# A transformer decoder on one core: rotary products read from PSUM, layernorm's step on ScalarE, a re-priced plan, and the token shift by SBUF-to-SBUF transfers

## The chip, the cores and the metric

The kernel runs on one core of one Trainium2 chip. The metric is the device time of one execution in microseconds. Before the change the median of three runs is 1289.61 us (1286.52 to 1293.66). The profile is one further execution, which took 1292.12 us, with a span of 1290.3 us from its first to its last instruction.

## The reference

`x` and a context have 32 batches of 128 tokens by 128 channels, all fp32. Four stages follow one another, with a layernorm after the first, the second and the last two together:

```
x = layernorm(x + self_attention(x))              # 16 heads, keys = queries = x
x = layernorm(x + cross_attention(x, ctx))        # 16 heads of 8, band mask of width 64
x = layernorm(x + layer_1(layer_0(x)))            # two local-attention layers

def shift_token(t):                               # half of the channels one token later
    t1, t2 = split(t, 2, axis=-1)
    t2 = pad(t2, one row of zeros ahead)[:, :-1]
    return concatenate([t1, t2])

def layer(x):
    h = shift_token(x)
    q, k, v = split(h @ wqkv, 3)                  # 8 heads of 64
    q, k = l2norm(q) * qs, l2norm(k) * ks
    q, k = rotary(q, k)                           # q * cos * scale + rotate_half(q) * sin * scale
    x = x + local_attention(q, k, v) @ wo
    h = layernorm(shift_token(x)) * lg + lb
    a, g = split(h @ w1 + b1, 2)
    return x + (a * gelu(g)) @ w2 + b2
```

What the change touches is `shift_token`, used twice in each layer, the rotary step with the norms of q and k, and every layernorm.

## The kernel before

**Tiling.** The 32 batches are cut into ten groups of 2, 3, 3, 4, 4, 4, 4, 4, 3 and 1 (`SIZES`); n is the number of batches in a group. Tokens lie on the 128 partitions, so a group's tile is 128 x (n x 128) elements. Each group goes through four stages: self attention (`self_attention`), cross attention (`cross_attention`), layer 0 and layer 1 (`layer`). Each stage works batch by batch, and the stages of different groups are mixed with each other, each stage a set lag behind the one before (`LAGS`, `CLOSE`, `SPREAD`, `EARLY`).

**What sets the order.** Nothing is issued while it is described. `op` (L84) notes down an engine, a price in ns, what is read and written, and the function that emits it. At the end `Plan.issue` (L132) makes a list schedule: it keeps a clock for each engine, reckons when each ready operation could start from the prices of what it needs, and takes the operation of least number among those that can start within `NEAR` ns of the earliest. The result is one fixed order for each of the engines PE, DVE, ACT, POOL and SP. Every engine then runs its own order, waiting at each instruction for what it needs. The prices exist only in this plan; they decide the order, and nothing on the chip. Buffers come from rings (`Ring`): `m` is the eight PSUM banks, `big` and `mid` are SBUF tiles, `sm` small ones. Transfers all go through SP's queue; a transfer is priced at 1800 ns before it moves, its bytes over a rate, and 400 ns after it.

**The token shift.** `shifted` (L759), used ahead of each layer's feed-forward part, makes a shifted tile in SBUF: POOL copies the first 64 channels (L763), TensorE multiplies the other 64 by a shifted identity matrix (L767), which moves rows one partition on and puts a zero in the first, and ScalarE copies the result out of PSUM (L771). `turned_shifted` (L774), at the start of each layer, needs the shifted tile transposed. It transposes the plain tile (L373), and ScalarE copies the second half one column on (L782, L783), where a column of zeros has been set by POOL (L779).

**A local batch.** `local_batch` (L790) takes one batch through a layer's attention. TensorE makes q, k and v (L796). ScalarE copies each out of PSUM (L801) and squares q and k (L807); VectorE sums the squares (L810); POOL takes the power -1/2 (L813, L814). POOL multiplies the swapped halves by the sine table (L824), VectorE the plain ones by the cosine table (L833), adds the two (L837), and scales by the norms (L840). Transposes (L851), scores (L865, L871), maxima (L421), exponentials (L466), the division (L885, L886), transposes of the weights (L481, copied at L488), the outputs (L900) and the projection (L912) follow; L919 adds the result to x.

**Layernorm** (L377): VectorE's statistics (L382, L389), POOL's power (L397 to L400), and one scaling per batch on VectorE (L407).

**Copies of transposed weights.** `turned_half` (L475) transposes four heads and copies them out of PSUM (L488): on VectorE in cross attention, on ScalarE in the layers.

**DMAs.** Besides weights and inputs, the scores of the first two stages pass through a DRAM scratch: `in_slots` writes each batch's three bf16 parts in pieces of 256 B from 128 partitions (L518), and `stacked` reads them back as 72 rows of 4096 B (L529).

Of the kernel before, what the change touches and what calls it, by code (L numbers as in the profile page):

```python
# [28 lines left out]
AHEAD = 430  # L29
LAGS = (0, 1.35, 2.75, 4.1)  # L30
RINGS = (23, 16, 6, 4)
KEEP = (2, 3, 5)
NEAR = 0
EARLY = (0, 0.2)
CLOSE = (0.9, 0.85, 0.9, 1, 1, 1, 1.2, 1.05, 0.85, 0.95)
SPREAD = (1.4, 1.0, 0.7, 1.5)
# [40 lines left out]
class Plan:  # L77

# [51 lines left out]
    def issue(self, ahead, near=80.0, hop=60.0, table_ns=1300.0, tiling_ns=160.0, dma_ns=1800.0):  # L132
# [13 lines left out]
        def time_of(k):  # L146
            e = ops[k][0]
            return max([0.0] + [end[d] + (hop if ops[d][0] != e else 0.0) for d in ops[k][3]])
# [5 lines left out]
        shared = 0.0  # L154
# [5 lines left out]
        while len(order) < n:  # L160
            best = None
            for e in engines:
                choice, least = [], None
                for k, t in ready[e]:
                    if k > first + ahead:
                        continue
                    start = max(clock[e], t, shared if ops[k][7] else 0.0)
# [5 lines left out]
                    for vs in need.values():  # L173
                        q = vs[0].ring
                        if len(q.free) < len(vs) + (0 if q.queue[q.head] in vs else q.keep):
                            ok = False
                            break
                        start = max(start, sorted(q.free)[len(vs) - 1][0] + hop)
# [4 lines left out]
                    if e == "PE" and ops[k][8][0] != state:  # L183
                        start += tiling_ns
# [19 lines left out]
            if e == "SP":  # L204
                line = max(line, s + dma_ns) + ns
                end[k], clock[e] = line + 400.0, s + 450.0
            else:
                end[k] = clock[e] = s + ns
            if tab:
                table[e] = tab  # L210
            if port:
                shared = end[k]
# [19 lines left out]
def decoder_kernel(ctx: ExitStack, tc: tile.TileContext, a: dict, out: bass.AP):  # L232
# [35 lines left out]

    ident1 = const.tile([P, P + 1], F32, name="ident")
    ident, shift = ident1[:, 1 : P + 1], ident1[:, 0:P]  # L270
    nc.vector.memset(ident1[:, 0:1], 0.0)
# [90 lines left out]
    def turned(src, n):  # L362

        tp, t = Val(mring), Val(mid)
        op("PE", 113 * n, turn(src, tp, n), [src], [tp], hold=[t])
        op("ACT", 140 + 113 * n,
           lambda: nc.scalar.copy(t.t[:, 0 : 128 * n], tp.t[:, 0 : 128 * n]), [tp], [t])
        return t
# [8 lines left out]
    def layernorm(src, dst, n):  # L377
# [6 lines left out]
        op("DVE", n * 290, stats, [src], [st])  # L384
# [6 lines left out]
        op("DVE", n * 175, aggr, [st], [mv])  # L391
# [10 lines left out]
        op("POOL", 1100 + 260 * n, rest, [], [mv])  # L402

        def apply():
            x, y = group(src.t), group(dst.t)
            for j in range(n):
                nc.vector.tensor_scalar(  # L407
                    y[:, j, :], x[:, j, :], mv.t[:, 8 + j : 9 + j], mv.t[:, 12 + j : 13 + j],
                    ALU.mult, ALU.add,
                )  # L410

        op("DVE", 200 * n, apply, [mv] + ([src] if src is not dst else []), [dst])
# [4 lines left out]
    def maxima(s, nm):  # L417
        for b in range(2):
            op(
                "DVE", 690,  # L420
# [5 lines left out]
    def minus_max(s):  # L426
# [6 lines left out]
        def parts():  # L433
# [4 lines left out]
        op("POOL", 440, parts, [nm], [hl])  # L438
        mp = Val(mring, lambda t: t[:, 0:64].bitcast(BF16))
        op(  # L440
            "PE", 110,
# [4 lines left out]
        op("ACT", 260, lambda: nc.scalar.copy(mT.t, mp.t), [mp], [mT])  # L446
# [10 lines left out]
    def exps_of(s, sums=None):  # L457
# [4 lines left out]
        for b in range(2):  # L462
# [8 lines left out]
            op("ACT", 4 * (345 if sums else 255) + 60, exps, [s[b], (nm, b)],  # L471
# [3 lines left out]
    def turned_half(e, et, b, eng, src):  # L475
# [9 lines left out]
        op("PE", 4 * 113, pe, [src], [tp], hold=[et])  # L485
        copy = nc.vector.tensor_copy if eng == "DVE" else nc.scalar.copy
        op(eng, 690 if eng == "DVE" else 590,
# [6 lines left out]
    def in_slots(src, n, keep_src, moving):  # L494
# [4 lines left out]
        op("ACT", 140 + 113 * n,  # L499
           lambda: nc.scalar.copy(pv.t[:, 0, every], src.t[:, every]), [src], [(pv, 0)])  # L500
        op("POOL", 316 * n,
# [3 lines left out]
        op("ACT", 140 + 113 * n,  # L505
           lambda: nc.scalar.copy(pv.t[:, 1, every], rest.t[:, every]), [rest], [(pv, 1)])
        op("POOL", 316 * n,
# [26 lines left out]
    def scores_of(s, stationary, moving, hh, window=False):  # L534
# [12 lines left out]
        op("PE", 8 * 62 + 432 * window, pe,  # L547
# [22 lines left out]
    def self_half(j, hh, x0, xT, ys):  # L570
# [3 lines left out]
        for b in range(2):  # L574
# [3 lines left out]
                "PE", 875,  # L578
# [6 lines left out]
                "ACT", 590,  # L585
# [10 lines left out]
        op("PE", 8 * 60, lambda: emit_max(s, mT), [mT, (w_self, 2)], s)  # L596
        e = Val(big, heads)
        for b in range(2):
            op("ACT", 590,
# [3 lines left out]
        for k, (h0, n) in enumerate(((0, 3), (3, 3), (6, 2))):  # L603
# [9 lines left out]
            op("PE", 230 * n, pe, [e] + [(zs, i) for i in range(3)], [oz])  # L613
# [9 lines left out]
            op("DVE", 175 + 30 + 133 * n, scale, [oz], [rl, (zs, ("o", k))])  # L623

        z = lambda h0, n: zs.t[:, h0 : h0 + n, 0:D]
        for n, ns in ((4, 1270), (2, 730), (1, 450)):
# [4 lines left out]
        op("POOL", 450,  # L631
# [4 lines left out]
    def cross_attention(g):  # L636
# [9 lines left out]
        for w, src, c in ((wqT, xT, 0), (wkT, cT, 1)):  # L646
            qp, t = Val(mring), Val(mid)
            op("PE", 20 + 214 * n,
# [3 lines left out]
            op("ACT", 265 + 106 * n,  # L652
# [16 lines left out]
        op("PE", n * 228, values, [cT, w_cross], [vp], hold=[vT])  # L669
        op("ACT", 140 + 113 * n,  # L670
           lambda: nc.scalar.copy(vT.t[:, every], vp.t[:, every]), [vp], [vT])
        op("POOL", 316 * n,
# [21 lines left out]
        op("PE", n * 228, project, [onT, w_cross], [yp])  # L694
        op("DVE", 160 + 135 * n,
# [7 lines left out]
    def cross_batch(j, qs, ks, vT, on):  # L703
        vb = Val(vbring)
        op("POOL", 450,
# [5 lines left out]
        for hh in range(2):  # L711
# [4 lines left out]
            for b in range(2):  # L716
                turned_half(e, et, b, "DVE", e)
# [13 lines left out]
            op("PE", 875, pe, [et, vb], [o], hold=[oS], tiling=("columns", "columns"))  # L731
            op("ACT", 260,
# [11 lines left out]
        op("PE", 260, back, [oS], [ot])  # L744
# [11 lines left out]
        op("DVE", 560, normal, [ot], [rl, (on, j)])  # L756


    def shifted(src, n):  # L759

        h = Val(mid)
        op("POOL", 200 * n,
           lambda: nc.gpsimd.tensor_copy(group(h.t)[:, 0:n, 0:64], group(src.t)[:, 0:n, 0:64]),  # L763
           [src], [(h, 0)])
        sp = Val(mring, lambda t: t[:, 0 : 64 * n].rearrange("p (g d) -> p g d", g=n))
        op("PE", 25 + 111 * n,
           lambda: nc.tensor.matmul(  # L767
               sp.t, shift, group(src.t)[:, 0:n, 64:128], start=True, stop=True),
           [src], [sp], hold=[h])
        op("ACT", 180 + 53 * n,  # L770
           lambda: nc.scalar.copy(group(h.t)[:, 0:n, 64:128], sp.t), [sp], [(h, 1)])  # L771
        return h

    def turned_shifted(src, n):  # L774

        tp, t = Val(mring), Val(mid)
        op("PE", 113 * n, turn(src, tp, n), [src], [tp], hold=[t])
        op("POOL", 150,
           lambda: nc.gpsimd.memset(group(t.t)[64:128, 0:n, 0:1], 0.0), [], [(t, 0)])  # L779

        def act():
            nc.scalar.copy(t.t[0:64, 0 : 128 * n], tp.t[0:64, 0 : 128 * n])  # L782
            nc.scalar.copy(  # L783
                group(t.t)[64:128, 0:n, 1:P], group(tp.t)[64:128, 0:n, 0 : P - 1]
            )

        op("ACT", 280 + 225 * n, act, [tp], [(t, 1)])
        return t

    def local_batch(l, j, xin, hT, xout):  # L790
        qk = Val(big, lambda t: t[:, 0:1024].rearrange("p (a d) -> p a d", d=LD))
        vs = Val(mid, lambda t: t[:, 0:512].rearrange("p (h d) -> p h d", d=LD))
        for i in range(3):
            hp = Val(mring)
            op("PE", 875,
# [3 lines left out]
               [hT, w_layer[l]], [hp], hold=[qk if i < 2 else vs])  # L799
            op("ACT", 590,  # L800
               lambda hp=hp, i=i: nc.scalar.copy(  # L801
                   qk.t[:, LH * i : LH * (i + 1), :] if i < 2 else vs.t,
                   hp.t.rearrange("p (h d) -> p h d", d=LD)),
               [hp], [(qk, i) if i < 2 else vs])

        sq = Val(big, lambda t: t[:, 0:1024].rearrange("p (a d) -> p a d", d=LD))
        op("ACT", 1060, lambda: nc.scalar.activation(sq.t, qk.t, AF.Square), [qk], [sq])  # L807
        rn = Val(small)
        op("DVE", 1225,
           lambda: nc.vector.tensor_reduce(rn.t[:, 0:16], sq.t, AX.X, ALU.add), [sq], [rn])  # L810
# [7 lines left out]
        four = lambda t: t[:, 0:1024].rearrange("p (a h d) -> p a h d", a=2, d=LD)  # L818
        r2 = Val(big, four)

        def swap():
            q = qk.t.rearrange("p (a h) d -> p a h d", a=2)
            for d0, d1 in ((0, 32), (32, 0)):
                nc.gpsimd.tensor_tensor(  # L824
                    r2.t[:, :, :, d0 : d0 + 32], q[:, :, :, d1 : d1 + 32],
                    tabs[l][:, :, d0 : d0 + 32].unsqueeze(2).to_broadcast([P, 2, LH, 32]),
                    ALU.mult,
                )

        op("POOL", 2600, swap, [qk, w_layer[l]], [r2], port=True)  # L830
        qr = Val(big, four)
        op("DVE", 1240,
           lambda: nc.vector.tensor_tensor(  # L833
               qr.t, qk.t.rearrange("p (a h) d -> p a h d", a=2),
               tabc[l].unsqueeze(2).to_broadcast([P, 2, LH, LD]), ALU.mult),
           [qk, w_layer[l]], [qr], port=True)
        op("DVE", 1240, lambda: nc.vector.tensor_tensor(qr.t, qr.t, r2.t, ALU.add), [r2], [qr], port=True)  # L837
        op("POOL", 3200, power, [], [rn])
        op("DVE", 1240,
# [5 lines left out]
        for i in range(2):  # L845
# [9 lines left out]
            op("PE", 4 * 113, pe, [qr], [tp], hold=[qkT])  # L855
            op("ACT", 590,
# [19 lines left out]
        op("PE", 1520, scores, [qkT, (w_self, 2)], s, tiling=("whole", "rows"))  # L876
# [4 lines left out]
        for b in range(2):  # L881
# [8 lines left out]
            op("DVE", 870, divide, [], [(rl, b), (e, b)], port=True)  # L890
# [15 lines left out]
        op("PE", 875, outputs, [et, vs], [o], hold=[onT], tiling=("columns", "columns"))  # L906
        op("ACT", 590, lambda: nc.scalar.copy(onT.t[:, 0:512], o.t), [o], [onT])
# [9 lines left out]
        op("PE", 4 * 228, project, [onT, w_layer[l]], [yp], hold=[xout] if xout is not xin else [])  # L917
        op("DVE", 290,
# [4 lines left out]
    def feed_forward(l, xg, n):  # L923
        every = slice(0, 128 * n)
        h = shifted(xg, n)
        op("POOL", 316 * n,
# [6 lines left out]
        op("PE", 113 * n, turn(h, tp, n), [h], [tp], hold=[hT])  # L933
        op("DVE", 160 + 135 * n,
# [188 lines left out]
```

## Time and profile before

| | us |
|---|---|
| median of the runs | 1289.61 |
| the profiled execution | 1292.12 |
| its span | 1290.3 |

| line | engine, what | count | busy us | mean ns |
|---|---|---|---|---|
| L421 | VectorE, maxima, 512 out of PSUM | 384 | 245.6 | 681 |
| L488 | VectorE, copy of transposed weights | 128 | 82.0 | 681 |
| L488 | ScalarE, copy of transposed weights | 128 | 75.0 | 598 |
| L600 | ScalarE, exponentials, 512 out of PSUM | 128 | 70.6 | 607 |
| L466 | ScalarE, exponentials, 128 out of PSUM | 1024 | 323.0 | 399 |
| L813 | POOL, power of 16 columns | 64 | 200.8 | 3137 |
| L407 | VectorE, layernorm's step, other three row groups | 96 | 40.9 | 400 to 536 |
| L771 | ScalarE, copy of the shifted half | 20 | 7.0 | 350 |
| L782, L783 | ScalarE, the two copies of the shifted transpose | 40 | 20.0 | 504, 493 |
| L367 | ScalarE, copy of a plain transpose | 20 | 10.5 | 523 |
| L763, L779 | POOL, copy and memset of the shift | 40 | 11.4 | 478, 98 |

How to read it: a row of the profile is a group of instructions by line, engine and operation. After the operation it names the tile written and those read, the shape, and the count; then the busy time in us and the mean duration of one in ns; then the idle time of that engine just before these instructions, and what ended it. TensorE's matmul rows of fp32 stand twice for one matmul, and consecutive ones overlap, so their mean is longer than the distance from start to start. A copy's duration likewise runs a little into the next instruction. The first stretches of the span have a busy DMA (0.86 over the first 100 us); later the DMA share falls to 0.15 and under.

The DMA queue of SP carried 173792 packets and 89.67 MB, 27.5% of the time of the core's 16 DMA engines.

### The profile page before, as it was taken

Reading aid. Unit: us, or ns where it says so; the run is one execution under the profiler, and the core shown is the slowest. Engines: PE = TensorE matmul, PEld = TensorE weight load, DVE = VectorE, ACT = ScalarE, POOL = GpSimd, SP = SyncE. Lnnn points to the kernel's source line nnn. Section 1 sums busy time; section 2 is a strip of 40 time slices with the busy share of each in tenths; the row PEclk is TensorE's granted clock in tenths of the full one; section 3 lists DMA queues with packets and bytes.
Section 4 is the critical chain, followed back from the end, with each engine's and each line's share of the span. In section 5 each row is a group of like instructions: output and inputs, shape, how many; then the busy total and the mean of one; then the engine's idle time right before and its main releaser. Section 6 shows DMA issues by size and latency. Waiting matters only on the chain.

```text
span 1290.3 us, 27579 instructions
## 1 busy us (share of the span) xinstructions
PE 1213.9 (94%) x9730; PEld 888.0 (69%) x9730; DVE 1070.3 (83%) x2134; ACT 966.2 (75%) x2762; POOL 835.3 (65%) x1094
## 2 busy tenths in 40 slices
PE   7988999999979999999999999999999989999996
PEld 4766677776767865777777667778667657567664
DVE  2677889878968888887798889979899999988786
ACT  4564777777867778777778778858889968879863
POOL 2866657765857389555687468653966963786454
PEclk9999999999989999999999999999999989999999
DMA  9886414240154420732005401330300000000000
GB/s 254 209 213 193 124 39 105 56 128 9 37 136 109 99 56 1 174 89 65 20 25 138 124 1 34 94 95 18 97 2 12 18 18 2 9 1 2 2 1 25
DMA packets 173930, 91.44 MB, mean 71 GB/s; under 512 B 155872, under 2 KB 161888, under 8 KB 173536
## 3 DMA queue, kind: packets, MB, share of 16 engines
q1 hardware_dynamic: 173792, 89.67, 27.5%
q8 instruction: 77, 1.26, 0.4%
q14 instruction: 61, 0.50, 0.1%
HBM read 49.79 MB, written 39.85 MB: 69 GB/s over the span
## 4 chain that ended last, share of the span: by engine, by line
PE 45%; POOL 15%; DVE 14%; ACT 6%; issue 3%; DMA 1%; SPq 0%; POOLq 0%; DVEq 0%; ACTq 0%
PE m L796 6%; POOL sm L813 6%; PE m L481 5%; PE m L944 4%; PE m L608 4%; ACT big L466 3%; PE m L900 3%; PE m L579 3%; PE m L871 3%; PE m L912 3%; POOL big L824 3%; PE m L964 3%; PE m L724 2%; DVE sm L421 2%; PE m L542 2%
## 5 line engine op out<-in xcount | busy, mean ns | idle before, releaser
L466 ACT ACTIVATE big<-m,sm 128x128 f32<-128x128 f32 x1024 | 323.0, 399 | 54.5 <-DVE sm L421 53.9
L421 DVE TENSOR_REDUCE sm<-m 128x4 f32<-128x512 f32 x384 | 245.6, 681 | 45.4 <-PE m L871 21.5
L813 POOL TENSOR_TENSOR sm<-sm,nhalf 128x16 f32<-128x16 f32 x64 | 200.8, 3137 | 36.8 <-DVE sm L810 26.7
L628 POOL TENSOR_TENSOR big<-big 128x512 f32<-128x512 f32 (+2 forms) x192 | 163.2, 850 | 83.8 <-DVE big L618 36.8
L824 POOL TENSOR_TENSOR big<-big,layer_w 128x512 f32<-128x512 f32 x128 | 162.4, 1269 | 76.4 <-ACT big L801 71.1
L796 PE MATMUL m<-layer_w,mid 128*128 128x512 f32 x384 | 193.2, 612 | 4.2 <-DVE xb L971 2.1
L481 PE MATMUL m<-ident,big 128*128 128x128 f32 x1024 | 144.4, 276 | 15.4 <-DVE big L886 9.6
L481 PEld LDWEIGHTS m<-ident,big 128*128 128x128 f32 x1024 | 115.7, 141 | 54.9 <-issue 21.9
L579 PE MATMUL m<-self_w,mid 128*128 128x512 f32 x256 | 131.1, 626 | 7.0 <-DMA self_w<-in_self_w 5.7
L608 PEld LDWEIGHTS m<-big,big 128*128 128x128 f32 x1024 | 123.0, 191 | 13.7 <-issue 7.5
L608 PE MATMUL m<-big,big 128*128 128x129 f32 x1024 | 129.9, 276 | 0.9 <-DVE big L618 0.3
L466 ACT ACTIVATION_READ_ACCUMULATOR big<-m,sm 128x1 f32 x512 | 115.9, 226 | 0.0
L586 ACT COPY big<-m 128x512 f32<-128x512 f32 x128 | 75.1, 600 | 38.8 <-PE m L579 38.0
L618 DVE TENSOR_TENSOR big<-m,sm 128x384 f32<-128x384 f32 (+1 forms) x192 | 98.6, 514 | 6.6
L886 DVE TENSOR_TENSOR big<-big,sm 128x512 f32<-128x512 f32 x128 | 98.2, 767 | 4.6 <-DMA slots<-big 0.2
L542 PEld LDWEIGHTS <-big 72*128 72x128 bf16 x1024 | 72.3, 98 | 41.3 <-issue 20.2
L542 PE MATMUL m<-big,big 72*128 72x128 bf16 x1024 | 87.8, 220 | 9.6 <-DMA big<-slots 8.9
L488 ACT COPY big<-m 128x512 f32<-128x512 f32 x128 | 75.0, 598 | 28.3 <-PE m L481 19.4
L796 PEld LDWEIGHTS m<-layer_w,mid 128*128 128x128 f32 x384 | 64.7, 193 | 42.6 <-issue 27.9
L857 ACT COPY big<-m 128x512 f32<-128x512 f32 x128 | 71.6, 608 | 29.7 <-PE m L851 29.1
L944 PE MATMUL m<-mid,layer_w 128*128 128x512 f32 (+7 forms) x240 | 89.5, 516 | 2.7 <-DVE mid L935 1.5
L488 DVE COPY big<-m 128x512 f32<-128x512 f32 x128 | 82.0, 681 | 11.5 <-PE m L481 10.7
(116 smaller groups left out, 2611.4 us busy)
## 6 DMA issues: line engine op xcount, KB each, us to landing
slots<-big SPq DMA_DIRECT2D x384, 96.0 KB
big<-slots SPq DMA_DIRECT2D x128, 288.0 KB
layer_w<-in_layer_w SPq DMA_DIRECT2D x2, 1877.0 KB
mid<-in_xt SPq DMA_DIRECT2D x5, 256.0 KB
mid<-in_xg SPq DMA_DIRECT2D x5, 256.0 KB
mid<-in_ct SPq DMA_DIRECT2D x5, 256.0 KB
out<-xb SPq DMA_DIRECT2D x5, 256.0 KB
self_w<-in_self_w SPq DMA_DIRECT2D x2, 512.0 KB
```

Of the source, the lines that this page charges most:

```text
L421: lambda b=b: nc.vector.tensor_reduce(nm.t[:, 4 * b : 4 * b + 4], s[b].t, AX.X, ALU.max, negate=True),
L466: nc.scalar.activation(e.t[:, h, :], s[b].t[:, h - 4 * b, :], AF.Exp, bias=nm.t[:, h : h + 1], accum_out=sums.t[:, h : h + 1] if sums else ...
L481: nc.tensor.transpose(tp.t[:, 128 * c : 128 * c + 128], e.t[:, 4 * b + c, :], ident)
L488: lambda: copy(et.t[:, 4 * b : 4 * b + 4, :], tp.t.rearrange("p (c k) -> p c k", c=4)),
L542: nc.tensor.matmul(s[b].t[:, i, :], st[:, h, :], mv[:, h, :], start=not window and i == 0, stop=i == 3,)
L579: lambda zp=zp, h0=h0: nc.tensor.matmul(zp.t, group(xT.t)[:, j, :], attn_w[:, h0 : h0 + 4, :], start=True, stop=True),
L608: nc.tensor.matmul(oz.t[:, i, :], e.t[:, h0 + i, :], zs.t[:, h0 + i, :], start=True, stop=True,)
L628: lambda n=n: nc.gpsimd.tensor_tensor(z(0, n), z(0, n), z(n, n), ALU.add),
L796: lambda hp=hp, i=i: nc.tensor.matmul(hp.t, group(hT.t)[:, j, :], wqkv[l][:, INNER * i : INNER * (i + 1)], start=True, stop=True),
L813: nc.gpsimd.tensor_tensor(rn.t[:, 0:16], rn.t[:, 0:16], nhalf, ALU.pow)
L824: nc.gpsimd.tensor_tensor(r2.t[:, :, :, d0 : d0 + 32], q[:, :, :, d1 : d1 + 32], tabs[l][:, :, d0 : d0 + 32].unsqueeze(2).to_broadcast([P, ...
L944: lambda t=t, off=off, c0=c0, m=m: nc.tensor.matmul(t.t[:m, every], w1[l][:, off + c0 : off + c0 + m], hT.t[:, every], start=True, stop=True),
```

## The change

**The shift.** Both shifts become one function that makes a tile in SBUF by two transfers on SP's queue: the first 64 channels stay on their partitions, the other 64 go one partition on; POOL zeroes the first row. The second transfer has 127 rows. `turned_shifted` is gone: a layer begins with a plain transpose of the shifted tile.

```diff
 def shifted(src, n):
     h = Val(mid)
-    op("POOL", 200 * n, lambda: nc.gpsimd.tensor_copy(group(h.t)[:, 0:n, 0:64], group(src.t)[:, 0:n, 0:64]), ...
-    op("PE", 25 + 111 * n, lambda: nc.tensor.matmul(sp.t, shift, group(src.t)[:, 0:n, 64:128], ...
-    op("ACT", 180 + 53 * n, lambda: nc.scalar.copy(group(h.t)[:, 0:n, 64:128], sp.t), [sp], [(h, 1)])
+    op("POOL", 60, lambda: nc.gpsimd.memset(group(h.t)[0:1, 0:n, 64:128], 0.0), [], [(h, 0)])
+    for late in range(2):
+        c = slice(64 * late, 64 * late + 64)
+        op("SP", P * 256 * n / 190,
+           lambda c=c, late=late: nc.sync.dma_start(
+               group(h.t)[late:P, 0:n, c], group(src.t)[0 : P - late, 0:n, c]),
+           [src], [(h, 1 + late)])
     return h
...
-    hT = turned_shifted(xin, n)
+    hT = turned(shifted(xin, n), n)
```

**Rotary and squares from PSUM.** q and k are no longer copied. ScalarE squares each half of 512 elements where TensorE left it, and VectorE makes the cosine product (one instruction of 512 elements) and the sine product of the swapped halves (two of 256) from there. POOL's product is gone; the sum, the power and the scaling stay.

```diff
-            op("ACT", 590, lambda hp=hp, i=i: nc.scalar.copy(qk.t[:, LH * i : LH * (i + 1), :] ...
-        op("ACT", 1060, lambda: nc.scalar.activation(sq.t, qk.t, AF.Square), [qk], [sq])
-        op("POOL", 2600, swap, [qk, w_layer[l]], [r2], port=True)
-        op("DVE", 1240, lambda: nc.vector.tensor_tensor(qr.t, qk.t..., tabc[l]..., ALU.mult), ...
+            op("ACT", 478, lambda hp=hp, i=i: nc.scalar.activation(sq.t[:, i], hp.t, AF.Square), ...
+            def rotate(hp=hp, i=i):
+                nc.vector.tensor_tensor(qr.t[:, i], hp.t, tabc[l][:, i]..., ALU.mult)
+                for d0, d1 in ((0, 32), (32, 0)):
+                    nc.vector.tensor_tensor(r2.t[:, i, :, d0 : d0 + 32], hp.t[:, :, d1 : d1 + 32], tabs[l]..., ALU.mult)
+            op("DVE", 598 + 2 * 335, rotate, [hp, w_layer[l]], [(qr, i), (r2, i)])
```

**Layernorm's step and half of the copies.** Both go to ScalarE:

```diff
-                nc.vector.tensor_scalar(y[:, j, :], x[:, j, :], mv.t[:, 8 + j : 9 + j], ..., ALU.mult, ALU.add)
+                nc.scalar.activation(y[:, j, :], x[:, j, :], AF.Identity, scale=mv.t[:, 8 + j : 9 + j], bias=...)
...
-                turned_half(e, et, b, "DVE", e)
+                turned_half(e, et, b, ("DVE", "ACT")[b], e)
```

**The plan.** Nearly all prices are other numbers (a copy on ScalarE 478 instead of 590, scores 1467 instead of 1520). In place of one hop of 60 ns the plan has, for each engine, a time after an instruction until its result is there (`TAIL`), a time to reach another engine (`HOP`) and one to follow on the same engine (`SELF`). In place of one shared clock for operations marked `port`, POOL's start after VectorE's last marked one, and marked ones of VectorE after POOL's last marked one. The constants of the order are others as well:

```diff
-AHEAD = 430
-LAGS = (0, 1.35, 2.75, 4.1)
-RINGS = (23, 16, 6, 4)
-KEEP = (2, 3, 5)
-NEAR = 0
+AHEAD = 290
+LAGS = (0, 1.35, 2.75, 4.2)
+RINGS = (21, 18, 6, 6)
+KEEP = (2, 3, 6)
+NEAR = 80
```

The order of all engines therefore changes from the first group on, not only around the shift.

## The prediction

> **What bounds the kernel now.** I read the page first: shares of busy time, then the chain that ended last, then the rows of the touched lines, then stretches of the span.
>
> ```profile
> span 1290.3 us, 27579 instructions
> ...
> PE 1213.9 (94%) x9730; PEld 888.0 (69%) x9730; DVE 1070.3 (83%) x2134; ACT 966.2 (75%) x2762; POOL 835.3 (65%) x1094
> ...
> PE 45%; POOL 15%; DVE 14%; ACT 6%; issue 3%; DMA 1%; SPq 0%; POOLq 0%; DVEq 0%; ACTq 0%
> ```
>
> TensorE is busy for 94%, yet carries only 45% of the chain: it is nearly full, and what holds it up is short waits on its neighbours, POOL foremost (15%, 194 us). The kernel is a pipeline whose engines all run in an order fixed when it is built. No engine may be late for long: TensorE has eight PSUM banks to run ahead into, a few us of work.
>
> ```profile
> L824 POOL TENSOR_TENSOR big<-big,layer_w 128x512 f32<-128x512 f32 x128 | 162.4, 1269 | 76.4 <-ACT big L801 71.1
> ...
> L833 DVE TENSOR_TENSOR big<-big,layer_w 128x1024 f32<-128x1024 f32 x64 | 86.0, 1343 | 3.9 <-ACT big L801 3.8
> L801 ACT COPY big<-m 128x512 f32<-128x512 f32 x128 | 75.1, 616 | 18.3 <-PE m L796 18.0
> ...
> L807 ACT ACTIVATE big<-big 128x1024 f32<-128x1024 f32 x64 | 69.1, 1079 | 1.1
> ...
> L407 DVE TENSOR_SCALAR mid<-mid,sm 128x128 f32<-128x128 f32 x64 | 31.4, 546 | 8.2 <-POOL sm L400 8.2
> ...
> L618 DVE TENSOR_TENSOR big<-m,sm 128x256 f32<-128x256 f32 x64 | 27.2, 425 | 2.2
> ...
> L767 PE MATMUL m<-xb,ident 128*128 128x256 f32 (+3 forms) x40 | 11.4, 367 | 0.5 <-DVE xb L919 0.4
> ```
>
> These are the rows that the change touches, and one (L618) that prices a new operation. The shift's matmul (L767) is tiny.
>
> **Rotary and squares.** For each of 64 local batches, POOL's L824 goes: -162.4 us. VectorE loses L833 (-86.0) and gains, for each of 128 halves, one product of 512 elements out of PSUM (the maxima, L421, take 681 ns at that size) and two of 256 (L618's form, 425 ns): 128 x 1531 ns = +196.0. ScalarE loses the q and k copies and the wide square (-75.1 - 69.1) and gains 128 squares at 607 ns (L600's mean): +77.7.
>
> **Layernorm's step.** 160 instructions of L407, 72.3 us over its four row groups (31.4 + 15.3 + 14.6 + 11.0), leave VectorE; on ScalarE each is near an exponential of the same size (L466, 399 ns): +63.8.
>
> **Half of the cross copies.** 64 copies of L488: -43.6 on VectorE (681 ns), +38.3 on ScalarE (598 ns).
>
> **The shift.** TensorE -11.4 (L767). POOL loses 9.6 (L763) and 1.8 (L779), and gains 40 memsets at about 98 ns (L779's mean), 3.9. ScalarE loses 7.0 + 10.1 + 9.9 (L771, L782, L783) and gains 20 plain copies at 523 ns (L367), 10.5. SP gains 80 transfers.
>
> Sums: TensorE -11, VectorE +196.0 - 86.0 - 72.3 - 43.6 = -6, ScalarE +19, POOL -170. No engine becomes the bound by its load. What it is worth: the 11 us of TensorE give about 8 in its pipelined pitch (109 to 111 ns per block of 128 columns, the difference of starts among rows of that size, 64 blocks, and a little per group). L824 carries 3% of the chain (39 us); I give half of it back to what stands next on POOL, the power of L813 (6%). So **-27 us**; the ends are 0 and -60 (all of L824, and a plan with measured prices that fills part of TensorE's 76 us idle).
>
> **A wait that the plan does not see.** ScalarE's square and VectorE's three products now read the same PSUM bank. The trace before has no two engines reading one bank for independent work: the maxima come before the exponentials, which need them. The Trainium skill (PSUM — Partial Sum Buffer, section "PSUM bank collisions raise a hardware error") says two engines must not be in one bank at once, reads included. In the order of the changed kernel about half of the first products also wait for ScalarE, and about half of the squares for VectorE (part of these may be for a buffer's reuse). So the pair takes 607 + 1531 = 2138 ns, not 1531: either VectorE idles 0.6 us or ScalarE 1.5 us, up to 128 times. ScalarE has 25% idle, which covers most; with the cover gone it is 128 x 0.6 = 77 us. I take **+20**, ends 0 and 77.
>
> **What decides: one of the two transfers starts at partition 1.** A shift is two transfers on SP's queue: columns 0 to 63 over 128 partitions, and columns 64 to 127 from partitions 0..126 to 1..127. Nothing in the trace has 127 rows. Nearest rows:
>
> ```profile
> 1030.00:1031.00 1.00, 1.00 (x7) 0.67 (x6) 0.97 (x3) 1.00 (x8) 0.92 (x2) 1.00 0.81 188
> 1032.30:1034.80 2.50, 2.50 (x25) 1.96 (x25) 2.47 (x3) 2.44 (x6) 2.50 (x1) 1.00 0.69 208
> ```
>
> The last two columns are the DMA share and GB/s. The very first load, from the timeline (start, duration):
>
> ```profile
> 0.73 0.40 SPq L326 DMA_DIRECT2D mid<-in_xt  x1
> ...
> 2.94 0.41 ACT L500 CAST big<-mid 128x256 bf16<-128x256 f32 x1 [0.93 <-DMA mid<-in_xt]
> ```
>
> In the first stretch only 128-row transfers in pieces of 256 B run: 0.81 x 16 engines x 1000 ns / (188,000 B / 256 B) = 17.6 ns of one engine per piece. *By that row*, a shift of four batches is 512 pieces over 16 engines: 0.6 us. *By the rule* (the Trainium skill, DMA: Bandwidth & Descriptors, section "Why a DMA increments its semaphore by 16 and not by 1"): a transfer is spread over the largest number of engines, up to 16, that divides its outermost dimension, and 127, a prime, leaves **one** engine. Then it is 127 x 4 x 17.6 ns = 8.9 us. The second stretch speaks for the rule: there the 72-row transfers (L529) run alone, and the share sticks at 0.69, under 12/16; 12 is the largest divisor of 72 up to 16. I take the rule.
>
> From issue to use the first load took 2.94 - 0.73 = 2.2 us, some 0.5 of it moving (128 KB at 254 GB/s), so 1.7 us are fixed. The second transfer is issued 0.45 us after the first (L1001's issue is 0.45). It lands 0.45 + 1.7 + 2.235 n us after the producer, for n batches: 11.1, 8.9, 6.6, 4.4 for n = 4, 3, 2, 1. The plan reckons 2.2 + 0.345 n (450 to the second issue, 1800, two times 172 n, 400 at the end): 3.6, 3.2, 2.9, 2.5. Late by 7.5, 5.6, 3.7 and 1.9. Four shifts per group, groups of 2, 3, 3, five of 4, 3, 1: 4 x (3.7 + 3 x 5.6 + 5 x 7.5 + 1.9) = **240 us** of lateness.
>
> Is it hidden? Before, the same way (L919 to the first statistics) goes through three queues but needs only 1.3 us at best. In the changed order VectorE's statistics of the shifted tile mostly stand 1 to 5 us of its own work behind the producing addition, since the plan expects them to be ready: VectorE, in order, then stands still with everything behind it (maxima, products, copies that free PSUM banks), and TensorE with it. The other 20 shifts feed TensorE's own transposes. Each lateness is longer than TensorE's few us of cover, and adjacent shifts queue on the same DMA engine. I put 65% on the path: **+155**; ends 35% (85) and 90% (215). The loads of the scores' operands that stand behind on that engine I count at nothing: the one-engine transfers total 128 x 127 x 17.6 ns = 286 us of some 1400, and loads are mostly issued 10 to 80 us ahead; without that lead each would add up to 9 us.
>
> Sum against the profiled execution's own 1292.1 us (span 1290.3, 1.8 around it; the median of the runs is 1289.6): 1292 - 27 + 20 + 155 = **1440 us**.
>
> **Rivals.** *A, the forecast, 0.78*: 1330 to 1520. *B, faster, 0.13*: the transfer is spread over 16 engines after all (or its pieces go much faster inside SBUF). Landing is then 2.8 us after the producer, as planned, and the shift costs nothing: 1292 - 27 = 1265, with the bank wait 1285; 1240 to 1285. It decides where the 127-row transfer takes under about 1 us per batch: the lateness then falls under 3 us and into the cover. For it: POOL's large share of the chain is relieved. Against: the 0.69. *C, 0.05*: one engine, but other groups' work covers it: 20% of 240 on the path, 1292 - 27 + 20 + 48 = 1333 with the bank wait, 1313 without, down to 1290 with the larger gain. Against it: the few us between producer and statistics. *D, 0.04*: spread, but the bank wait at its full 77 and little gain, 1295 to 1365; for it the last 290 us, where VectorE is as full as TensorE:
>
> ```profile
> 1000.00:1100.00 100.00, 91.37 (x705) 64.93 (x701) 92.87 (x156) 79.58 (x250) 65.72 (x59) 0.97 0.05 12
> 1100.00:1200.00 100.00, 92.37 (x641) 63.13 (x642) 89.41 (x143) 86.01 (x238) 72.49 (x62) 1.00 0.01 4
> ```
>
> (TensorE, weight loads, VectorE, ScalarE, POOL). That the change does something else is out: the built order has the 80 transfers and no product on POOL.
>
> **Numbers.** A and most of C and D are slower: 0.83; B is faster but for its edge: 0.13; same 0.04 (0.5%, 6.5 us, is about what the runs before, 1286.5 to 1293.7, can tell from no change). Range 1290 to 1520: A, C and D; B stays out.
>
> **What would show it.** Right: the costliest waits name the shifted tile's transfer, before the statistics and before the transposes on TensorE, several us each and growing with n; TensorE's share falls to about 85%. POOL's busy time falls by some 170 us, VectorE's stays, ScalarE's rises by some 20. Wrong: no such waits, or of 1 to 2 us, and TensorE above 94%.

## The result, and the profile after

The changed kernel takes 1408.94 us (median of four runs, 1404.66 to 1414.18), against 1290.83 us for the kernel before in the same session: a ratio of 1.0912, with a 95% interval of 1.0882 to 1.0941. It is 118 us slower. The forecast was 1440 us, within 1290 to 1520.

The page of the changed kernel, first its busy shares, then the chain that ended last by engine and by line:

```profile
span 1412.4 us, 27767 instructions
...
PE 1243.7 (88%) x9656; PEld 905.9 (64%) x9690; DVE 1030.0 (73%) x2229; ACT 974.0 (69%) x2880; POOL 654.4 (46%) x966
...
PE 44%; DVE 20%; DMA 15%; ACT 8%; POOL 5%; issue 4%; SPq 3%; DVEq 0%; POOLq 0%; ACTq 0%
DMA mid<-xb 11%; PE m L617 6%; PE m L490 5%; PE m L787 5%; PE m L929 4%; ACT big L475 3%; PE m L588 3%; DVE sm L430 3%; PE m L856 3%; PE m L897 3%; DVE big L804 2%; PE m L551 2%; DVE big L800 2%; PE m L733 2%; PE m L949 2%
```

Every engine has a smaller share than before. POOL's part of the chain fell from 15% to 5%, and its work by 181 us. DMA rose from 1% to 15%, and the chain's costliest line is the shifted tile, `mid<-xb`. The transfers are not many, nor do they add much load (the DMA queue's share of the engines rose from 27.5% to 28.0%). They are long. The waits before the statistics of layernorm (L391; the tile read is the shifted one) show who stands still:

```profile
  DMA mid<-xb: 102.7, 20
```

That is VectorE's idle time until the transfer landed, and the number of times: all twenty feed-forward shifts, 5.1 us each in the mean. One of them, with four batches, in the chain in order of time (start, duration, what):

```profile
1323.71 0.29 DVE xb L904
1324.02 0.66 SPq L775
1324.73 9.20 DMA mid<-xb
1334.02 0.87 DVE sm L391 x4
...
1376.10 0.57 SPq L775
1376.72 7.45 DMA mid<-xb
...
1392.95 0.54 SPq L775
1393.55 3.69 DMA mid<-xb
```

L904 adds the attention's result, SP issues the 128-row transfer and then the 127-row one, and 9.20 us after the second issue began the tile has landed and the statistics start. With three batches the same way takes 7.45 us, with one 3.69: 1.84 us for each batch more, or 14.5 ns for each of its 127 pieces of 256 B. The stretches below, both inside such a transfer, say how it is carried. The columns are the stretch, its length, the busy time of TensorE, weight loads, VectorE, ScalarE and POOL, the granted clock, the DMA share and GB/s:

```profile
1326.00:1333.00 7.00, 4.75 (x12) 2.15 (x12) 1.90 (x5) 3.91 (x20) 0.75 (x2) 0.76 0.08 17
1233.50:1239.00 5.50, 5.38 (x30) 2.74 (x26) 1.03 (x2) 3.52 (x18) 0.00 (x0) 1.00 0.07 16
```

A share of 0.07 to 0.08 of sixteen engines is one engine (0.0625) whose pieces overlap a little: late in the first stretch's transfer they start 14 ns apart and take 18 ns each. The rate is 16 to 17 GB/s. In the first stretch VectorE worked 1.90 of 7.00 us, TensorE 4.75, and the granted clock was 0.76.

### The profile page after: what moved, and what is told of

The parts are those of the page before. It is cut to its first block, busy times and chain, and to the rows that moved or that the text cites. A ratio compares the mean times of both kernels' runs of the same rounds, so it can differ in the third digit from the quotient of the medians.

```text
span 1412.4 us, 27767 instructions
## 1 busy us (share of the span) xinstructions
PE 1243.7 (88%) x9656; PEld 905.9 (64%) x9690; DVE 1030.0 (73%) x2229; ACT 974.0 (69%) x2880; POOL 654.4 (46%) x966
## 4 chain that ended last, share of the span: by engine, by line
PE 44%; DVE 20%; DMA 15%; ACT 8%; POOL 5%; issue 4%; SPq 3%; DVEq 0%; POOLq 0%; ACTq 0%
DMA mid<-xb 11%; PE m L617 6%; PE m L490 5%; PE m L787 5%; PE m L929 4%; ACT big L475 3%; PE m L588 3%; DVE sm L430 3%; PE m L856 3%; PE m L897 3%; DVE big L804 2%; PE m L551 2%; DVE big L800 2%; PE m L733 2%; PE m L949 2%
## 5 line engine op out<-in xcount | busy, mean ns | idle before, releaser
L787 PE MATMUL m<-layer_w,mid 128*128 128x512 f32 x384 | 207.1, 649 | 32.7 <-DVE big L627 18.6
L490 PE MATMUL m<-ident,big 128*128 128x128 f32 x1024 | 152.4, 285 | 31.0 <-DVE big L871 24.2
L490 PEld LDWEIGHTS m<-ident,big 128*128 128x128 f32 x1024 | 120.3, 146 | 79.5 <-issue 26.2
L497 ACT COPY big<-m 128x512 f32<-128x512 f32 x192 | 116.8, 624 | 57.0 <-PE m L490 54.9
L617 PE MATMUL m<-big,big 128*128 128x129 f32 x1024 | 135.6, 286 | 8.7 <-DVE mid L760 3.7
L617 PEld LDWEIGHTS m<-big,big 128*128 128x128 f32 x1024 | 128.6, 200 | 22.1 <-issue 6.4
L795 ACT ACTIVATE big<-m 128x512 f32<-128x512 f32 x128 | 77.1, 631 | 58.2 <-PE m L787 30.5
L800 DVE TENSOR_TENSOR big<-m,layer_w 128x512 f32<-128x512 f32 x128 | 87.3, 682 | 19.6 <-ACT big L795 11.4
L391 DVE BATCH_NORM_STATS2 sm<-mid 128x6 f32<-128x128 f32 x96 | 21.8, 281 | 104.4 <-DMA mid<-xb 102.7
L912 POOL TENSOR_TENSOR xb<-xb,layer_w 128x512 f32<-128x512 f32 (+3 forms) x20 | 18.2, 909 | 171.4 <-DMA mid<-xb 164.1
L595 ACT COPY big<-m 128x512 f32<-128x512 f32 x128 | 74.8, 615 | 30.9 <-PE m L588 30.3
```

The costliest lines, as they stand in the source:

```text
L490: nc.tensor.transpose(tp.t[:, 128 * c : 128 * c + 128], e.t[:, 4 * b + c, :], ident)
L497: lambda: copy(et.t[:, 4 * b : 4 * b + 4, :], tp.t.rearrange("p (c k) -> p c k", c=4)),
L617: nc.tensor.matmul(oz.t[:, i, :], e.t[:, h0 + i, :], zs.t[:, h0 + i, :], start=True, stop=True,)
L787: lambda hp=hp, i=i: nc.tensor.matmul(hp.t, group(hT.t)[:, j, :], wqkv[l][:, INNER * i : INNER * (i + 1)], start=True, stop=True),
L800: nc.vector.tensor_tensor(qr.t[:, i], hp.t, tabc[l][:, i].unsqueeze(1).to_broadcast([P, LH, LD]), ALU.mult)
```

## Experiments

Twelve kernels were run besides the change. Times are medians; a ratio is to the kernel before in the same session, with its 95% interval.

| kernel | us | ratio |
|---|---|---|
| the change | 1408.9 | 1.0912 (1.0882 to 1.0941) |
| 127 rows cut into 112 + 15 | 1279.3 | 0.9918 (0.9887 to 0.9950) |
| change with TensorE's shift | 1310.2 | 1.0138 (1.0103 to 1.0174) |
| late transfer of 112 rows | 1276.8 | 0.9891 (0.9860 to 0.9922) |
| late transfer of 113 rows | 1392.3 | 1.0785 (1.0754 to 1.0817) |
| before with the two transfers | 1479.1 | 1.1453 (1.1414 to 1.1492) |
| before with the cut transfers | 1355.8 | 1.0493 (1.0463 to 1.0524) |
| change, true price in the plan | 1332.3 | 1.0316 (1.0263 to 1.0369) |
| cut, plan told of the bank | 1313.0 | 1.0165 (1.0132 to 1.0198) |
| before, AHEAD 420 | 1304.0 | 1.0125 (1.0071 to 1.0178) |
| before, the change's constants | 1340.9 | 1.0411 (1.0360 to 1.0463) |
| cut, AHEAD 300 | 1318.2 | 1.0235 (1.0184 to 1.0286) |
| TensorE's shift, AHEAD 300 | 1294.8 | 1.0045 (1.0014 to 1.0075) |

### Is it the 127 rows?

Only the late transfer is cut in two; the plan issues the same operations in the same order. (In the two traces the instructions of TensorE, VectorE, ScalarE and POOL are the same, one after the other.)

```diff
-               lambda c=c, late=late: nc.sync.dma_start(
-                   group(h.t)[late:P, 0:n, c], group(src.t)[0 : P - late, 0:n, c]),
+               lambda c=c, late=late: [nc.sync.dma_start(
+                   group(h.t)[r0 + late : r1 + late, 0:n, c], group(src.t)[r0:r1, 0:n, c])
+                   for r0, r1 in (((0, P),) if not late else ((0, 112), (112, 127)))],
```

> The changed kernel, with the 127-row transfer cut into one of 112 rows and one of 15; the plan and its order are the same. Theory (one DMA engine carries 127 rows): both pieces spread over 15 or 16 engines, land some 3 us after the producer, and nearly all of the 118 us over the kernel before goes, and the gain of the other parts shows: 1240 to 1300 us, statistics' wait for the transfer under 20 us in all. Rival (transfers inside SBUF, or 80 more of them on SP's queue, are slow as such): 1390 to 1430, as changed. Rival (the bank shared by ScalarE and VectorE, or the new plan, cost the time): 1340 or more.

1279.3 us: all 118 us are gone, and 12 more. The page of this kernel, and its waits before the statistics:

```profile
span 1276.7 us, 27843 instructions
...
PE 1201.4 (94%) x9656; PEld 878.2 (69%) x9690; DVE 1028.4 (81%) x2229; ACT 970.1 (76%) x2880; POOL 654.7 (51%) x966
```

```profile
  DMA mid<-xb: 11.6, 8
```

VectorE's wait for the shifted tile fell from 102.7 to 11.6 us. The number of instructions of TensorE is the same to a record (x9656), but its busy time is 42 us less. The kernel has 40 transfers more than the change, so neither the number of transfers nor the work of issuing them was the cost.

### One row

The sharpest form of the question: the late transfer with 112 rows and with 113, all else equal, transfers as many as in the change. 112 is divisible by 16; 113 is a prime.

```diff
-   op("POOL", 60, lambda: nc.gpsimd.memset(group(h.t)[0:1, 0:n, 64:128], 0.0), [], [(h, 0)])
+   op("POOL", 60, lambda: nc.gpsimd.memset(group(h.t)[:, 0:n, 64:128], 0.0), [], [(h, 0)])
...
-   group(h.t)[late:P, 0:n, c], group(src.t)[0 : P - late, 0:n, c]
+   group(h.t)[late : late + (P, 113)[late], 0:n, c], group(src.t)[0 : (P, 113)[late], 0:n, c]
```

> The changed kernel with the late transfer cut to 112 rows and POOL's memset over all rows, so the last 15 tokens' shifted half is left at zero; as many transfers as in the change. Theory (the number of DMA engines is the largest divisor of the rows up to 16): 16 engines, 1240 to 1300 us, each late transfer at 0.6 us for four batches. Rival (transfers as such): 1380 or more.

> The same with one row more, 113, a prime: the last 14 tokens' shifted half is left at zero. Theory: one engine again, 113/127 of the change's transfer time, 1370 to 1410 us, over 80 us slower than with 112 rows. Rival (transfers as such, or any other cause): within 10 us of the run with 112 rows.

One row more costs 115.5 us (1276.8 to 1392.3). The wait before the statistics with 112 rows, and the same wait in the list of waits with 113:

```profile
  DMA mid<-xb: 8.9, 7
```

```profile
DVE sm L391 <- DMA mid<-xb: 80.1, 20, 7.5
```

So it is not the bytes, the pieces, the place of the transfer or its start at partition 1. Two stretches inside the transfers of a four-batch shift, first with 112 rows, then with 113 (DMA share and GB/s last):

```profile
1204.50:1206.00 1.50, 1.07 (x11) 0.71 (x8) 1.50 (x3) 1.18 (x5) 1.39 (x2) 1.00 0.73 161
```

```profile
1308.00:1314.00 6.00, 3.14 (x12) 1.65 (x12) 1.70 (x5) 4.23 (x20) 0.55 (x2) 1.00 0.08 17
```

The 0.08 is one engine again, the 0.73 nine times as much. What is left is whether the number of rows can be divided among the DMA engines. Counts between the two extremes, as 126 or 120, were not run.

### The shift alone, on the kernel before

The kernel before gets `shifted` of the change (in the second run with 112 + 15 rows), and nothing else.

```diff
-        hT = turned_shifted(xin, n)
+        hT = turned(shifted(xin, n), n)
```

> The kernel before with the change's two shift transfers alone (127 rows in one of them), old plan and prices else. Theory: the late transfer costs here what it costs in the change, some 115 us as between 112 and 113 rows: 1380 to 1450. Rival (it costs so much only in the change's order, with few batches ahead): under 1340.

> The same with the late transfer cut into 112 and 15 rows. Theory (a well spread transfer is worth about as much as TensorE's shift): 1275 to 1300 us. Rival (the transfers relieve TensorE, ScalarE and POOL so much that this alone explains 1279 us of the split change): under 1280; then the other parts are worth nothing.

1479.1 and 1355.8 us; the first is above the 1380 to 1450 expected. Their difference, 123 us, is the third measurement of the same cost, in another kernel and another order (the same for both): 130 (the change against the cut), 115 (113 rows against 112), 123. But the cut transfers alone were expected at 1275 to 1300 us, and came 65 us above the kernel before. The wait for the tile is small there too:

```profile
  DMA mid<-xb: 13.0, 10
```

so the 65 us are not VectorE's wait before the statistics. Against the kernel before, TensorE was idle for 44 us more (120 against 76) and busy for 18 us more (1232.2 against 1213.9). Another suspect is POOL: it adds the feed-forward part's last bias to x in place, and cannot begin before the transfers have read x. Its wait in the list of waits (us, times, longest):

```profile
POOL xb L909 <- DMA mid<-xb: 92.2, 12, 30.7
```

Whether these waits or the other order cost the 65 us is not told apart. The next runs bear on it.

### All other parts of the change alone

Here the change keeps TensorE's shift of the kernel before (`shifted` and `turned_shifted`, with their old prices).

> The changed kernel with the shift of the kernel before (TensorE's shifted identity, ScalarE's and POOL's copies) in place of the transfers: all other parts of the change alone. Theory: they gain about 10 to 30 us against the kernel before, so 1250 to 1285 us. Rival (bank wait or plan cost the time): 1300 or more.

1310.2 us, not 1250 to 1285: the other parts alone look like a loss of 19 us. Before this can be believed, one has to know what another order of the same instructions costs.

### Orders

One constant of the plan is moved a little, first in the kernel before, then in the cut kernel and in the change with TensorE's shift; in a further run the kernel before gets all constants of the change.

```diff
-AHEAD = 430
+AHEAD = 420
...
-AHEAD = 290
+AHEAD = 300
```

> The kernel before with one constant of the plan moved a little (AHEAD 420 for 430): the same instructions in another order. Theory (the constants were fitted to one plan, and any other order costs some per cent): 1300 to 1340 us. Rival (orders are worth about the same): within 6 us of 1291.

> The kernel before with all plan constants of the change (AHEAD, LAGS, RINGS, KEEP, NEAR, EARLY, CLOSE, SPREAD), old instructions and prices. Theory (constants fit one plan only): 1310 to 1370 us. Rival (the new constants are a gain in themselves): under 1285.

> The split kernel (1279 us) with AHEAD 300 for 290. Theory (fitted constants): 1290 to 1320 us. Rival: within 6 us of 1279.

> The changed kernel with TensorE's shift (1310 us) with AHEAD 300 for 290. It was never fitted, so a move can go either way. Theory: between 1285 and 1330 us, so its 19 us over the kernel before say little about the instructions. Rival (the new instructions are slow in any order): 1305 or more, within 6 us of 1310.

The kernel before loses 16 us by the small step and 53 by the other constants (which also change the numbers of buffers). The cut kernel loses 39 and the kernel with TensorE's shift gains 15; these two compare runs of different sessions, and by their ratios to the kernel before it is 41 and 12. Not one instruction differs in kind. So an order alone moved these kernels by 12 to 53 us, up as well as down. That the kernel before and the cut kernel lose because their constants had been fitted to them is likely, but not shown. Differences of that size between kernels whose orders differ say nothing about their instructions: this covers the 19 us of the other parts alone, and it may cover the 65 us of the cut transfers on the kernel before. The comparisons within one order (the change, the cut, 112 and 113 rows) are free of it.

### Would a plan that knows help?

> The changed kernel, 127 rows in one transfer, but its price in the plan is the measured one (900 ns and 1830 ns per batch after the issue), so that the order puts other work ahead of those that wait. Theory (the lateness hurts since the order does not know it): most of it is covered, 1285 to 1340. Rival (the transfer's length itself is on the path, or later transfers behind it on its engine): 1380 or more.

```diff
-            op("SP", P * 256 * n / 190,
+            op("SP", (P * 256 * n / 190, 1830 * n - 1300)[late],
```

With the true price the plan puts other work ahead of what waits: 1332.3 us, 77 us better with the same long transfers. The order is another one, so part of the 77 us can be chance, but the wait before the statistics is a fifth of what it was:

```profile
  DMA mid<-xb: 22.5, 14
```

It is still 53 us behind the cut kernel. Its order, too, was not fitted, so how much of these 53 us is the transfer and how much the order is not told apart.

### The bank with two readers

In the cut kernel, the row of ScalarE's squares and that of VectorE's first product:

```profile
L796 ACT ACTIVATE big<-m 128x512 f32<-128x512 f32 x128 | 77.2, 633 | 38.7 <-DVE big L805 23.1 <-PE m L788 15.2
...
L801 DVE TENSOR_TENSOR big<-m,layer_w 128x512 f32<-128x512 f32 x128 | 87.5, 683 | 18.5 <-ACT big L796 10.8 <-PE m L788 6.9 <-ACT big L609 0.4
```

By the profile's account ScalarE stood 23.1 us until VectorE was out of the bank, VectorE 10.8 us until ScalarE was. The plan was then told that the products follow the square:

```diff
-            op("DVE", 598 + 2 * 335, rotate, [hp, w_layer[l]], [(qr, i), (r2, i)])
+            op("DVE", 598 + 2 * 335, rotate, [hp, (sq, i), w_layer[l]], [(qr, i), (r2, i)])
```

> The split kernel, with the plan told that VectorE's products follow ScalarE's square of the same bank. Theory (the bank's two readers wait for each other and the plan does not know, some 39 us of idle time on the two engines in the changed kernel): 5 to 15 us less than the 1279 of the split kernel. Rival (ScalarE and VectorE have idle time to cover it): within 5 us of it, or slower since VectorE always comes second.

1313.0 us, 34 us slower than the cut kernel, not 5 to 15 us faster. The same two rows:

```profile
L801 DVE TENSOR_TENSOR big<-m,layer_w 128x512 f32<-128x512 f32 x128 | 87.4, 683 | 25.4 <-ACT big L796 23.5
...
L796 ACT ACTIVATE big<-m 128x512 f32<-128x512 f32 x128 | 78.7, 638 | 21.7 <-PE m L788 18.4
```

ScalarE no longer waits for VectorE, VectorE waits longer for ScalarE, and the idle time before the two rows fell from 57.2 to 47.1 us. So the loss is not in these waits. A step of AHEAD in the same kernel costs 39 us, and another order is enough to explain it. What the bank costs in time stays open; in the cut kernel the two waits come to 34 us, on engines that have more idle time than that.

## Why the prediction was right, and where its terms were off

**One DMA engine for 127 rows.** Right, and shown twice over: by the DMA share of 0.07 to 0.08 during a late transfer (0.73 with 112 rows), and by the one row between 112 and 113. The rule of the Trainium skill (DMA: Bandwidth & Descriptors, section "Why a DMA increments its semaphore by 16 and not by 1") that the prediction preferred to the 128-row transfers of the trace is the one that holds here, at 112, 113 and 127 rows; the weak sign for it, a share of 0.69 with 72 rows, is not contradicted, but no run here shows how many engines 72 rows use.

**240 us of lateness.** A little large. From the producer's end to the statistics the trace shows 10.0 us for four batches, 8.2 for three and 4.4 for one, where 11.1, 8.9 and 4.4 were reckoned: a piece takes 18 ns, as reckoned (17.6), but the next one starts 14 ns after it, and 14.5 ns per piece is what the landing grew by. The fixed part, from the second issue on, was near 1.8 us. The plan's own figures for two batches and one are 3.0 and 2.8 us by its code, not 2.9 and 2.5, and the terms listed for them do not add up to 2.2 + 0.345 n (the 450 ns are hidden behind the first transfer from three batches on); this alone takes 2 us off the 240. Taken through the same sum, with 6.3 for two batches, the lateness is 4 x (5 x 6.4 + 3 x 5.0 + 3.3 + 1.6) = 208 us.

**65% of it on the path.** The change against the cut kernel, same order: 1408.9 - 1279.3 = 130 us, which is 62% of 208. This was a choice between 35% and 90%, and a good one: of the 31 us by which the forecast was too high, 25 are here. But its picture was only half right. Both kinds of shift were expected to hold their engine up alike. At the statistics VectorE waited 102.7 us. At the transposes that begin a layer TensorE's rows show much less:

```profile
  issue: 27.2, 19
  ACT mid L416: 10.2, 18
  DMA mid<-xc: 9.8, 2
  DMA mid<-xb: 2.3, 1
```

12.1 us name the transfer. The "issue" of 27.2 us is less in the cut kernel:

```profile
  issue: 3.7, 13
```

So most of it belongs to the transfers as well, though the view does not name them. That makes some 35 us, a third of VectorE's. Why a layer's start was covered better was not tried.

**What the stalls cost besides.** The prediction took 155 us as idle time. Of the 136 us between the two profiled spans (1412.4 and 1276.7), 93 are TensorE's added idle time, and 42 are longer busy time of the same instructions (1243.7 against 1201.4). This is the clock, below, for which the prediction had no term. The idle time alone is 45% of the 208 us of lateness; that the clock's share brought the sum near the 65% was luck.

**Loads that stand behind, at nothing.** They were held up: 37 of SP's 638 issuing instructions took more than 1.5 us, 163 us together, against 13 of 678 and 26 us in the cut kernel. But the loads came early enough: TensorE waited 7.4 us for the scores' operands, in the cut kernel 5.1.

**-27 us for the other parts, +20 for the bank.** Their sum, -7, would put the kernel without late transfers at 1285 us; the cut kernel took 1279.3. The sum fits, but this may be luck: the runs on orders show that the time left over depends on the constants by more than these terms, and neither term is confirmed. POOL's load fell by 181 us (170 were reckoned), and its part of the chain with it.

**Loads.** New rows were priced well: the product out of PSUM took 682 ns (681), the halves 412 (425), the squares 631 (607). Layernorm's step on ScalarE took 488 to 511 ns, where 399 was taken. VectorE's busy time fell by 40 us, not 6. In part this is the way of counting: the three products come to 182 us of busy time, not 196, mostly since busy time counts overlapping instructions once and the sum of durations counts them twice. In part instructions that the change leaves alone got shorter (scaling by the norms 1251 instead of 1362 ns, the division 732 instead of 767, together 12 us); why was not tried, and the rest was not taken apart. ScalarE rose by 8 us, not 19. TensorE was reckoned at -11 us and shows +30; in the cut kernel, with the clock nearly full, it shows -12.5.

**Rivals.** B, the transfer spread over sixteen engines, was forecast at 1265 or, with the bank's wait, 1285: this is what the cut kernel is (1279.3), so the rival was well priced, and only the row count separated it from the change. C, covered by other work, is what the true price in the plan makes of it (1332.3, with 1333 forecast; so close a fit, in another order, is chance), but the change's plan did not know the price. TensorE's share fell to 88%, not 85%.

The cut kernel beats both: 0.9918 of the kernel before (0.9887 to 0.9950).

## What to carry to other kernels

Look at the row count of every transfer that does not begin at the first partition or end at the last: "all but one row" is 127, and both primes tried here, 127 and 113, put the transfer on one DMA engine. Cut it into counts that divide well, here 112 and 15; in this kernel that was worth 130 us, and the 40 added transfers cost nothing that showed. Where an order is fixed at build time, tell it the true latency: the same long transfers cost 130 us with the wrong price and 53 with the right one, the order's chance included in the second. And two kernels with different orders can't be compared to within some 50 us out of 1300: compare within one order, or move a constant and see.

## What was not expected of the hardware

TensorE's granted clock falls with its stalls. The view of cores gives the span and the mean of the granted clock, first for the cut kernel, then for the change:

```profile
core 0: 1276.7 us, clock 0.990
```

```profile
core 0: 1412.4 us, clock 0.948
```

In the clock's records of the traces it is either full or half, nothing between. A mean of 0.948 over 1412.4 us is 2 x 0.052 x 1412.4 = 147 us at half speed, against 2 x 0.01 x 1276.7 = 26 us in the cut kernel. Of the change's 24 stretches at half clock, 15 begin within 8 us of the end of one of the twenty waits for a shifted tile, and 4 more next to TensorE's waits at a layer's start. The wait shown above, in two parts, gives the order of the two (columns as in the first stretches):

```profile
1326.00:1329.30 3.30, 1.17 (x9) 0.98 (x9) 1.90 (x5) 3.23 (x18) 0.75 (x2) 0.98 0.07 16
1329.30:1333.00 3.70, 3.58 (x4) 1.16 (x4) 0.00 (x0) 0.68 (x2) 0.00 (x0) 0.56 0.08 18
```

First TensorE stands, at a clock of 0.98; then it works, at 0.56. The matmuls that make q, k and v, the same in number and shape, have these rows in the cut kernel and in the change:

```profile
L788 PE MATMUL m<-layer_w,mid 128*128 128x512 f32 x384 | 192.8, 610 | 6.0 <-DVE big L627 3.4
```

```profile
L787 PE MATMUL m<-layer_w,mid 128*128 128x512 f32 x384 | 207.1, 649 | 32.7 <-DVE big L627 18.6
```

In the change's trace a matmul of 512 columns took 606 ns in the mean at full clock (687 of them) and 1089 at half (40). TensorE was busy for 104 us of the time at half clock, in the cut kernel for 19; half of the difference is the 42 us by which its busy time is longer. So a stall of several us is paid for twice: in the wait, and in slower matmuls after it. The kernel before with the two transfers, whose TensorE is idle longest (215 us), has the lowest mean, 0.934. Between kernels the rule is only a rough one: the cut kernel whose plan was told of the bank has 0.971 with 88 us idle, TensorE's shift in the changed kernel 0.986 with 91.
